# Statistics, weight sums, aggregation, buffer order and top row in a windowed attention followed by a convolution

## The chip, the core and the metric

The kernel runs on one core of a Trainium2 chip. TensorE (PE) multiplies, VectorE (DVE), ScalarE (ACT) and GpSimd (POOL) do the work on elements, SyncE (SP) issues most of the transfers. Each engine takes its instructions in their order and waits for the others by semaphores. [...] The metric is the device time in microseconds, here the median of three runs.

## The reference, cut to what matters

```
x: (2, 128, 256, 256)
# layer 0: halo attention, windows of 8x8 queries, 12x12 keys, 4 heads of 32
x = x + attention(gn(x), W_qkv, W_out, rel_height, rel_width)
# layer 1
n = gn(x)
t1 = conv(n, w1 (128,128,5,1));  t3 = depthwise_conv(t1, w3, 3 rows)
t4 = sum over c and three columns (-2, 0, +2) of n * w4   # 8 groups
x = x + t4 * t3

gn(v): over 32 groups of 4 channels, (v - mean) / sqrt(var + 1e-5),
       mean and var over the group's 4 channels and all 256x256 pixels
```

A normalisation therefore needs the mean and variance of a whole image before its first element can be normalised. There are four: x0 and x1 (the inputs of the two images) and y0 and y1 (their sums after the attention).

## The kernel before, in words

The channels lie on the 128 partitions. An image is cut into 32 strips of 8 rows (`NS`), and the two images make 64 strips k. In the attention a strip is worked on in two units u = 2k and 2k+1, one for each parity of rows, 128 in all (`NU`). In the convolution a strip is one step.

**Setup (L225 to L253).** Constants are loaded, and all 32 strips of the first image come in through six buffers `f_sx`. VectorE takes statistics of each with four `bn_stats` (`Norms.chunk`), one for every two rows, into a table of 128 x 6 numbers. `normalise(0)` (L299) then calls `Norms.group`, which runs `Norms.steps` through: one `bn_aggr` over the whole table, a matmul with `gavg` that averages the channels of a group, small operations on VectorE, a second matmul, a square root on ScalarE and its reciprocal.

**Attention.** From L553 the order on each engine is the order of the program, written by hand. A unit is: biases, scores (L458, L474), values (L439, copied out by ScalarE and VectorE, L445), coefficients of the next strip (L418), attend (L499 to L506), turn (L517), then keys or queries of later units (L354, L393), then project (L533), which adds the input and stores the result from `f_x1` by SP (L537). In even units the next strip is normalised on VectorE (L322 to L328), and GpSimd sorts it into `f_xq` (L337). Every unit also takes statistics of the result before (`result_stats`).

While image 0 is worked on, image 1's input statistics are taken: `stats_at` says which strip in which unit. `load_next` loads it into the single buffer `f_sx`, one ahead, and `input_stats` runs four `bn_stats` at the start of the unit. The steps of a normalisation are spread over two units: `norm_at` starts x1 at u=61 and y0 at u=69, and `step()` runs one piece at a time. At u=8 VectorE prepares six sums of convolution weights (`Weights.sums`, L638).

**Passage to the convolution.** `convolutions_fast` is a generator. The last units of the attention call it for the first loads, the first normalised strip, its row sums and its `unfold` (L735, with five small transfers on SP, L754). Then the attention's pools close: `f_cst` with the constants, keys and values, `f_x1` with two result buffers, `f_wk` with the working tiles. The convolution opens `f_t1` and `f_wk1` on the same addresses. Pools stand one behind the other in the order in which they are opened, so a tile may have to wait for the last use of what lay there.

**Convolution (L894 on).** A strip is: `unfold` (L740) and `first_rows`, then `vertical` twice (L760, L799, results to VectorE L803, L810, L816), with the next strip's normalisation between (L684, L687, L688 on ScalarE, L727, L731 on VectorE), `depthwise` (L828), `spread` (L839) and `combine` (L849). The last image's aggregation y1 starts at k=3. Products go through four banks, `pj`, in turn.

## Time and profile before

| | us |
|---|---|
| median of three runs (3076.55 to 3078.32) | 3078.05 |
| the profiled execution | 3077.89 |
| its span, first to last instruction | 3076.00 |
| PE busy | 2950.9 (96%) |
| DVE busy | 2522.4 (82%) |
| ACT busy | 1732.8 (56%) |
| POOL busy | 657.8 (21%) |
| granted TensorE clock, mean | 0.998 |

The profile lists, for each engine and line, the busy time, and the idle time ahead of an instruction with what ended it. A row of the timeline reads: start, length, engine, line, operation, out<-in, shapes, count, and in brackets the idle time before it with its releaser. Several instructions of a line in succession are merged into one row. A busy TensorE is modelled, so gaps between the starts of the same step in successive units are the safer measure of its delays.

### The profile page before, as it was taken

The numbers are of one execution on the slowest core, as the hardware profiler recorded it, in microseconds if no ns is written. First come the engines' busy times: TensorE is split into PE (matmuls) and PEld (weight loads), VectorE is DVE, ScalarE is ACT, GpSimd is POOL, SyncE is SP. The second block draws the span as 40 slices with busy tenths as digits, with TensorE's granted clock in tenths as the row PEclk, the third lists the DMA queues.
The fourth block names the chain that finished last, engine by engine and source line by source line (L and its number), as shares of the span: only waits on it lengthen the run. The fifth ranks groups of instructions, "written<-read, shape, count | busy, mean of one in ns | idle before, by whom it ended". The sixth has DMA issues, their size and how long they took to land.

```text
span 3076.0 us, 116627 instructions
## 1 busy us (share of the span) xinstructions
PE 2950.9 (96%) x52090; PEld 2223.8 (72%) x52090; DVE 2522.4 (82%) x4092; ACT 1732.8 (56%) x2673; POOL 657.8 (21%) x1433
## 2 busy tenths in 40 slices
PE   0799999999999999999999999999999999999998
PEld 0688888888888888888888888884444444444443
DVE  8788888888888877777777777768999999999998
ACT  0455555555555655555555555555666665666664
POOL 2322232323232222323232323220000000000001
PEclk9999999999999999999999999999999999999999
DMA  9433333333333221222222222225788888888886
GB/s 393 167 126 126 114 117 113 116 113 116 112 117 113 85 72 65 89 72 90 73 90 73 90 72 89 73 96 141 209 222 221 215 210 217 216 217 216 217 216 167
DMA packets 137404, 434.78 MB, mean 141 GB/s; under 512 B 12992, under 2 KB 87616, under 8 KB 104384
## 3 DMA queue, kind: packets, MB, share of 16 engines
q1 hardware_dynamic: 127824, 361.18, 33.8%
q0 software_dynamic: 9072, 66.06, 11.7%
q8 instruction: 412, 6.75, 0.9%
q14 instruction: 96, 0.79, 0.1%
HBM read 284.59 MB, written 134.22 MB: 136 GB/s over the span
## 4 chain that ended last, share of the span: by engine, by line
PE 93%; DVE 2%; ACT 1%; issue 0%; POOL 0%; DMA 0%; SPq 0%; DVEq 0%; ACTq 0%
PE f_pv L439 15%; PE a_e L760 10%; PE a_o L760 10%; PE f_s L474 8%; PE f_o L499 8%; PE f_pk L354 8%; PE f_pq L393 7%; PE f_py L354 7%; PE f_pa L418 4%; PE f_s L458 4%; PE a_d L799 3%; PE b L839 2%; PE a_c L760 2%; PE g L740 2%; POOL f_xq L337 0%
## 5 line engine op out<-in xcount | busy, mean ns | idle before, releaser
L445 DVE COPY f_vt<-f_pv 64x512 f32<-64x512 f32 x512 | 354.2, 695 | 299.5 <-ACT f_vt L445 299.3
L337 POOL COPY f_xq<-f_xn 128x128 f32<-128x128 f32 x1024 | 399.2, 441 | 707.9 <-DVE f_xn L322 647.9
L439 PE MATMUL f_pv<-f_wqkvT,f_xn 128*128 128x128 f32 x4096 | 491.3, 278 | 0.0
L439 PEld LDWEIGHTS f_pv<-f_wqkvT,f_xn 128*128 128x128 f32 x4096 | 466.9, 192 | 8.6
L483 ACT ACTIVATE f_p<-f_s 128x512 f32<-128x512 f32 x512 | 264.5, 602 | 320.0 <-PE f_s L474 320.0
L399 ACT ACTIVATE f_q<-f_pq,f_head 128x512 f32<-128x512 f32 x512 | 303.1, 703 | 145.2 <-PE f_pq L393 145.2
L445 ACT COPY f_vt<-f_pv 64x512 f32<-64x512 f32 x512 | 298.2, 584 | 116.9 <-PE f_pv L439 116.5
L821 ACT ACTIVATE t<-t,w 128x1024 f32<-128x1024 f32 x128 | 146.9, 1148 | 372.4 <-DVE t L816 367.9
L828 DVE SCALAR_TENSOR_TENSOR t<-t,w,t 128x1024 f32<-128x1024 f32 x256 | 329.9, 1288 | 7.4 <-ACT t L821 1.3
L474 PEld LDWEIGHTS f_s<-f_q,f_kt 64*64 64x64 f32 x16384 | 250.9, 135 | 50.1 <-issue 49.9
L474 PE MATMUL f_s<-f_q,f_kt 64*64 64x64 f32 x16384 | 268.7, 220 | 0.6 <-issue 0.6
L367 ACT COPY f_kt<-f_pk 128x512 f32<-128x512 f32 x256 | 154.6, 604 | 196.4 <-PE f_pk L354 196.4
L499 PE MATMUL f_o<-f_vt,f_p 128*32 128x66 f32 x16384 | 263.6, 222 | 1.4 <-issue 0.7
L857 POOL DMA_DIRECT2D y<-f_x x63 | 54.7, 868 | 915.2 <-DVE y L849 900.2
L499 PEld LDWEIGHTS f_o<-f_vt,f_p 128*32 128x32 f32 x16384 | 241.9, 110 | 10.8 <-DVE f_cf L431 1.0
L354 PE MATMUL f_py<-f_ot,f_woT 128*128 128x256 f32 x1024 | 242.2, 379 | 2.2 <-DVE f_ot L517 2.2
L354 PE MATMUL f_pk<-f_xn,f_wqkvT 128*128 128x256 f32 (+2 forms) x1258 | 243.0, 345 | 0.0
L393 PE MATMUL f_pq<-f_xq,f_wq_s 128*128 128x256 f32 (+1 forms) x1370 | 240.5, 331 | 0.8 <-DVE f_rc L505 0.8
L313 POOL COPY f_xn<-f_xn 128x1280 f32<-128x1280 f32 x62 | 86.7, 1399 | 720.6 <-PE f_pv L439 720.6
L760 PE MATMUL a_e<-xm,w1s 128*128 128x512 f32 x512 | 240.7, 591 | 0.0
L760 PE MATMUL a_o<-xm,w1s 128*128 128x512 f32 x512 | 240.3, 590 | 0.0
L393 PEld LDWEIGHTS f_pq<-f_xq,f_wq_s 128*128 128x128 f32 x1370 | 208.2, 191 | 23.3 <-PE pv_x L141 0.4
(131 smaller groups left out, 4696.9 us busy)
## 6 DMA issues: line engine op xcount, KB each, us to landing
f_raw<-in_x SPq DMA_DIRECT2D x62, 1280.0 KB, 7.8
f_sx<-in_x SPq DMA_DIRECT2D x64, 1024.0 KB, 12.4
f_x<-f_x SPq DMA_DIRECT2D x128, 512.0 KB, 3.4
y<-f_x POOLq DMA_DIRECT2D x63, 1024.0 KB, 8.0
out<-y SPq DMA_DIRECT2D x63, 1024.0 KB, 4.4
raw<-f_x SPq DMA_DIRECT2D x64, 640.0 KB, 6.4
raw<-f_x SPq DMA_DIRECT2D x62, 384.0 KB, 6.5
t<-t4p SPq DMA_DIRECT2D x192, 32.0 KB, 4.7
```

The costliest lines, as they stand in the source:

```text
L337: nc.gpsimd.tensor_copy(xq[:, half, t2, :, :, c].rearrange("p t r n e -> p r t n e"), cells[:, :, 16 * half + c : 16 * half + 16 : 2, 1 + ...
L354: nc.tensor.matmul(dst[:, 512 * lo // last : 512 * hi // last], w, moving[:, n * lo // last : n * hi // last], start=True, stop=True,)
L367: nc.scalar.copy(cur[:, c, 1:129, 2:6], pk.rearrange("p (j i) -> p j i", i=4))
L393: nc.tensor.matmul(pq.rearrange("p (h n e t) -> p h t n e", h=2, n=8, e=2)[:, half, lo:hi], wq_s, xq[:, half, :, :, r, c].rearrange("p s t ...
L399: nc.scalar.activation(q[:, c, :, i], pq.rearrange("p (n x) -> p n x", n=NPAIR), AF.Copy, scale=head[:, i : i + 1],)
L439: nc.tensor.matmul(pv[:, P * n : P * n + P], xn[k % 2][:, r, 4 * j + n].rearrange("p c x -> p (c x)"), wvT, start=True, stop=True,)
L445: (nc.vector.tensor_copy if c else nc.scalar.copy)(vt[rows, 4 * j : 4 * j + 4, :, c, 0:32], pv[rows].rearrange("p (n h d) -> p n h d", n=4 ...
L474: nc.tensor.matmul(sc[g][n // 8][64 * c : 64 * c + 64, n % 8].rearrange("p i x -> p (i x)"), keys_k[rows, c, 48 * n : 48 * n + 64], qs[u][ ...
L483: nc.scalar.activation(pts[u][:, g, 8 * half : 8 * half + 8].rearrange("p n i x -> p (n i x)"), sc[g][half].rearrange("p n i x -> p (n i x ...
L499: nc.tensor.matmul(po[32 * h : 32 * h + 32, n - lo], p[:, h // 2, n, h % 2], vt[:, n, h], start=True, stop=True,)
L760: nc.tensor.matmul(pa[:, : n * W], w, rows, start=i == 0, stop=i == len(terms) - 1)
L828: nc.vector.scalar_tensor_tensor(t3[:, j : j + 4], t1[:, j + tap : j + tap + 4, :], w3[:, tap : tap + 1], t3[:, j : j + 4], ALU.mult, ALU.add,
```

## The change

Five edits:

1. Image 1's input statistics are taken in odd units only: ten rows each in the first eight, eight rows in the other twenty-two. Before, two strips fell on the even units 4 and 8. The buffer `f_sx` grows to ten rows. To make room, the first strip's `t4` moves from its own tile into the unused rows of `raws[0, -1]`.
2. The six weight sums run on GpSimd instead of VectorE.
3. The table of statistics is aggregated in four quarters. Three of each image's quarters are aggregated early: in the setup after strips 7, 15 and 23, in the attention at the ends of the units in `quarter_at`. The last is the first step of the normalisation, and the small operations combine the four.
4. The pool of the results, `f_x1`, is opened after the working pool `f_wk`.
5. For the first strip of the convolution the products of the top row are issued right after `unfold(0)`, ahead of the last projection, and their copy stays in `first_rows`.

```diff
@@ class Norms
+    def quarter(self, st, name, i):
+        if i == 0:
+            self.mvs[name] = self.glob.tile([P, 4, 2], F32, tag=f"mv_{name}", name=f"mv_{name}")
+        self.nc.vector.bn_aggr(
+            self.mvs[name][:, i], st[:, self.ns * i : self.ns * i + self.ns].rearrange("p n k -> p (n k)")
+        )
     def steps(self, st, ps_pool, name, tag="pj"):
-        mv = small.tile([P, 2], F32, tag="mv", name=f"mv_{name}")
-        nc.vector.bn_aggr(mv, st.rearrange("p n k -> p (n k)"))
+        self.quarter(st, name, 3)
+        mv = self.mvs[name]
         yield
...
-        nc.tensor.matmul(pm[:, 0:1], gavg, mv[:, 0:1], start=True, stop=True)
+        nc.tensor.matmul(pm[:, 0:4], gavg, mv[:, :, 0], start=True, stop=True)
         yield
...
-        nc.vector.tensor_copy(mean, pm[:, 0:1])
-        d = small.tile([P, 1], F32, tag="d", name=f"d_{name}")
-        nc.vector.tensor_sub(d, mv[:, 0:1], mean)
+        nc.vector.tensor_reduce(mean, pm[:, 0:4], AX.X, ALU.add)
+        nc.vector.tensor_scalar(mean, mean, 0.25, None, ALU.mult)
+        d = small.tile([P, 4], F32, tag="d", name=f"d_{name}")
+        nc.vector.tensor_scalar(d, mv[:, :, 0], mean, None, ALU.subtract)
+        nc.vector.tensor_mul(d, d, d)
+        nc.vector.tensor_add(d, d, mv[:, :, 1])
         q = small.tile([P, 1], F32, tag="q", name=f"q_{name}")
-        nc.vector.tensor_mul(q, d, d)
-        nc.vector.tensor_add(q, q, mv[:, 1:2])
+        nc.vector.tensor_reduce(q, d, AX.X, ALU.add)
...
-        nc.vector.tensor_scalar(v, pv[:, 0:1], 1e-5, None, ALU.add)
+        nc.vector.tensor_scalar(v, pv[:, 0:1], 0.25, 1e-5, ALU.mult, ALU.add)
@@ attention_fast, setup
                 norm.chunk(st_x[0], 4 * s, t)
+                if s % 8 == 7 and s < 31:
+                    norm.quarter(st_x[0], "x0", s // 8)
+        wk = l0.enter_context(tc.tile_pool(name="f_wk", bufs=2))
         x1p = l0.enter_context(tc.tile_pool(name="f_x1", bufs=2))
-        wk = l0.enter_context(tc.tile_pool(name="f_wk", bufs=2))
...
+        quarter_at = {}
         for b in range(NB - 1):
-            for s in range(NS - 2):
-                stats_at[2 * (b * NS + s) + 1] = b + 1, s
-            stats_at[2 * (b * NS + 2)] = b + 1, NS - 1
-            stats_at[2 * (b * NS + 4)] = b + 1, NS - 2
+            row = 0
+            for i in range(NS - 2):
+                n = 10 if i < 8 else 8
+                stats_at[2 * (b * NS + i) + 1] = b + 1, row, n
+                row += n
+            for i, u in enumerate((30, 46, 58)):
+                quarter_at[2 * b * NS + u] = st_x, b + 1, f"x{b + 1}", i
...
+        for b in range(NB):
+            for i, u in enumerate((34, 50, 66) if b + 1 < NB else (34, 42, 50)):
+                quarter_at[2 * b * NS + u] = st_y, b, f"y{b}", i
...
                 project(u)
                 step()
+                if u in quarter_at:
+                    st, i, name, part = quarter_at[u]
+                    norm.quarter(st[i], name, part)
@@ Weights.sums
-        self.nc.vector.tensor_add(self.w1s[:, 0], w[1], w[3])
-        self.nc.vector.tensor_scalar(self.w1s[:, 1], w[3], -1.0, None, ALU.mult)
+        self.nc.gpsimd.tensor_add(self.w1s[:, 0], w[1], w[3])
+        self.nc.gpsimd.tensor_scalar(self.w1s[:, 1], w[3], -1.0, None, ALU.mult)
         for i, (a, b) in enumerate(((2, 1), (4, 3), (0, 1), (2, 3))):
-            self.nc.vector.tensor_sub(self.w1s[:, 2 + i], w[a], w[b])
+            self.nc.gpsimd.tensor_sub(self.w1s[:, 2 + i], w[a], w[b])
@@ convolutions_fast
             if k == 0:
-                t4 = both.sb.tile([P, 2, W], F32, tag="t4", name=f"t4_{k}")
+                t4 = raws[0, -1][:, 0:2, :]
...
+        def top_row(k):
+            xt = xn[k % 2]
+            return taps(
+                f"{k}_first", 1,
+                [(w1[:, tap], xt[:, tap - 1 : tap, 2 : 2 + W]) for tap in (2, 3, 4)],
+            )
-        def first_rows(k):
+        def first_rows(k, top=None):
...
-                top = taps(
-                    f"{k}_first", 1,
-                    [(w1[:, tap], xt[:, tap - 1 : tap, 2 : 2 + W]) for tap in (2, 3, 4)],
-                )
-                nc.scalar.copy(t1[:, 1:2, :], top)
+                nc.scalar.copy(t1[:, 1:2, :], top_row(k) if top is None else top)
...
         unfold(0)
+        top = top_row(0)
         yield
...
-                first_rows(k)
+                first_rows(k, top if k == 0 else None)
```

More of the change, by code (lines that the diff above doesn't have):

```diff
@@ L111, in __init__ @@
         self.nc, self.glob, self.small, self.gavg, self.ns = nc, glob, small, gavg, ns
-        self.done = {}
+        self.done, self.mvs = {}, {}
     def new(self, name, tag):
@@ L274, in load_next @@
                 u = coming.pop(0)
-                b, s = stats_at[u]
-                sxs[u] = t = rawp.tile([P, 8, W], F32, tag="sx", name=f"f_sx_{b}_{s}", bufs=1)
-                nc.sync.dma_start(t, x[b, :, 8 * s : 8 * s + 8, :])
+                b, row, n = stats_at[u]
+                t = rawp.tile([P, 10, W], F32, tag="sx", name=f"f_sx_{b}_{row}", bufs=1)
+                sxs[u] = t[:, 0:n]
+                nc.sync.dma_start(sxs[u], x[b, :, row : row + n, :])
         def input_stats(u):
-            b, s = stats_at[u]
-            norm.chunk(st_x[b], 4 * s, sxs.pop(u))
+            b, row, n = stats_at[u]
+            norm.chunk(st_x[b], row // 2, sxs.pop(u))
         def load_rows(k):
@@ L666, in load_rows1 @@
             if s == 0:
-                pre = rawp.tile([P, 8, W], F32, tag="sx", name=f"raw1_{b}_pre", bufs=1)
+                pre = rawp.tile([P, 10, W], F32, tag="sx", name=f"raw1_{b}_pre", bufs=1)
                 nc.sync.dma_start(pre[:, 5:8, :], x1_d[b][0][:, 0:3, :])
@@ L761, in taps @@
             return pa[:, : n * W].rearrange("p (r w) -> p r w", w=W)
-        def first_rows(k):
+        def top_row(k):
[5 more added lines that the diff above has]
+        def first_rows(k, top=None):
             s = k % NS
-            xt = xn[k % 2]
             t3 = wk.tile([P, 8, W], F32, tag="t3", name=f"t3_{k}")
```

## Prediction

> **What bounds the kernel now.** The page comes first: it gives engine shares and the chain that ended last.

> ```profile
> PE 2950.9 (96%) x52090; PEld 2223.8 (72%) x52090; DVE 2522.4 (82%) x4092; ACT 1732.8 (56%) x2673; POOL 657.8 (21%) x1433
> PE 93%; DVE 2%; ACT 1%; issue 0%; POOL 0%; DMA 0%; SPq 0%; DVEq 0%; ACTq 0%
> ```

> TensorE carries the kernel, and the change removes no matmul. It can gain only where TensorE waits, so the waits and the timeline come next. The first matmuls of L458 mark the starts of the 128 units. Units last 15.31 to 15.35 us except at u=0 (16.49), 4 (16.17), 8 (19.89), 61 (16.87), 62 (18.09), 64 (16.2, four extra matmuls), 69 (16.86), 70 (16.55) and 126 (14.37). In the convolution the first matmuls of L740 mark strips of 15.17 us, except the first (19.68), second (16.84) and fifth (17.14).

> Timeline of u=8, then of odd unit 29, then of u=61:

> ```profile
> 239.43 2.46 DVE L119 BATCH_NORM_STATS2 st_x<-f_sx 128x6 f32<-128x512 f32 x4
> 242.35 1.71 DVE L644 TENSOR_TENSOR w1s<-w 128x128 f32<-128x128 f32 x4
> 244.93 1.88 PE L418 MATMUL f_pa<-f_xq,f_wb 128*64 128x64 f32 x32 [2.95 <-DVE f_vt L445]
> ...
> 562.31 2.46 DVE L119 BATCH_NORM_STATS2 st_x<-f_sx 128x6 f32<-128x512 f32 x4
> 566.54 0.69 DVE L445 COPY f_vt<-f_pv 64x512 f32<-64x512 f32 x1 [1.76 <-ACT f_vt L445]
> ...
> 1061.91 0.15 DVE L133 COPY mean_x<-pm_x 128x1 f32<-128x1 f32 x1
> 1063.53 3.73 PE L393 MATMUL f_pq<-f_xq,f_wq_s 128*128 128x256 f32 x22 [0.38 <-DVE f_rc L505]
> ```

> In even units, which also normalise a strip, VectorE's added work makes TensorE wait. After four statistics an odd unit still has 1.76 us of idle VectorE; without them it has 4.14. At u=61 the small operations stand ahead of f_rc, and the projection waits for them.

> Timelines of the setup and of the passage to the convolution:

> ```profile
> 42.49 47.37 DVE L119 BATCH_NORM_STATS2 f_st_x<-f_sx 128x6 f32<-128x512 f32 x76 [0.48 <-DMA f_sx<-in_x]
> 89.90 3.62 DVE L127 BATCH_NORM_AGGREGATE mv_x<-f_st_x 128x2 f32<-128x768 f32 x1
> ...
> 2083.24 1.96 PE L354 MATMUL f_py<-f_ot,f_woT 128*128 128x256 f32 x8 [1.47 <-DVE f_ot L517]
> 2085.04 1.46 PE L760 MATMUL a_first<-xm,w 128*128 128x256 f32 x6
> 2091.25 0.37 ACT L794 COPY both<-a_c 128x256 f32<-128x256 f32 x1 [4.30 <-DMA f_x<-f_x]
> 2102.36 0.70 PE L760 MATMUL a_c<-sm,w1s 128*128 128x256 f32 x2 [0.90 <-DVE c L803]
> 2141.09 3.61 DVE L127 BATCH_NORM_AGGREGATE mv_y<-st_y 128x2 f32<-128x768 f32 x1
> 2150.28 0.70 PE L760 MATMUL a_c<-sm,w1s 128*128 128x256 f32 x2 [1.31 <-DVE c L803]
> ```

> Setup: 75 steps between 76 statistics take 47.37-0.68 us, 0.623 each; in unit 29 they take (2.46-0.67)/3 = 0.597. So VectorE waits some 4 x 0.026 = 0.10 us per strip for the loads, whose windows show the DMA engines full (419 GB/s). It looks busy but is paced by transfers.

> [...] (1) [...] the smallest take 0.13 to 0.16 us. (2) [...] L828, 2.60 us for two, takes 4.02 beside GpSimd's L870. [...]

> **The change, part by part.** The sum stands against the profiled 3077.89 us (span 3076.00 and 1.89 around it), 0.16 below the median.

> 1. *Statistics in odd units only.* u=4 and u=8 lose 2.46 us of VectorE each. u=4 gains 16.17-15.33 = 0.84. Eight odd units get a fifth statistic, 0.60, under 1.76 of idle: 0 (uncovered, 8 x 0.60 = 4.8). SP loses two loads; the eight of 1.31 MB, 25% longer, are issued a pair of units (30.7 us) ahead, against 12.4 to landing, and the first stands behind the first two strips' rows: 0.

> 2. *Weight sums on GpSimd.* VectorE loses 0.27+0.43+1.71 at u=8. With part 1 its loss goes: 19.89-15.33 = 4.56. GpSimd queues the six ahead of f_xq, behind L313 which ends at 228.13; f_xq starts at 238.12, waiting for normalisation, so 9.99 us stand free. Dear bound: L871, 1.70 us for 256 elements, gives 6 x 1.70 = 10.2, 0.2 too long. [...] I take 0.

> Parts 1 and 2: -5.4.

> 3. *Aggregation in quarters.* By (1) a quarter costs between 3.61/4 = 0.90 and (3.61-0.16)/4+0.16 = 1.02; I take 0.95.
>  - Setup: three quarters go among the statistics. Each delays VectorE by 0.95, and the next eight strips win 0.8 back from its waits; 0.45 is left at the end. The next load is issued up to 1.25 us late, but a load takes 12.4 us to land, five strips of 2.5, so DMA keeps a queue. Then 0.95 replaces 3.62: 0.45+0.95-3.62 = -2.2. Two more small operations follow on the open chain, 0.19 each: +0.4. Sum -1.8. If every delay of VectorE delayed the loads too: 3 x 0.95+0.95-3.62+0.4 = +0.6. The first strip's rows landed at 90.45, so they are not late next.
>  - Attention: three quarters for x1 and six for y close even units; the following odd units' 1.76 or 4.14 cover them: 0 (uncovered, 9 x 0.95 = 8.6). At u=61 and 69 the whole aggregate was hidden (0.61 of idle after it), so shortening gives nothing, but the two extra operations stand ahead of f_rc, for which the projection waits: 2 x 0.4 = +0.8. The square roots at u=62 and 70 keep their loss.
>  - Convolution: the aggregate at 2141.09 cost the fifth strip 17.14-15.17 = 1.97, of which 0.31 is pm's own matmuls. A 0.95 operation stays inside the lead of 1.87 us that VectorE's c has in steady strips (c at 3045.80, a_c at 3047.67): -1.65.

> 4. *Results' buffers behind the others.* `both` is the first tile written in the convolution's working pool. That pool's addresses cover the buffers of f_x1, and its copy L794 starts 0.10 us after the last f_x store landed at 2091.15. By the tiles' sizes (45 KB of constants, 50 of wk, 8 of x1; 39 of t1, sm and df, 43 of wk1) the new pools end before x1's new place. L794 then follows a_c, near 2085.7. Behind it on ScalarE stand L684, L687 and L688, 5.0 us, done near 2091; VectorE's sums start after its t at about 2092.3 instead of 2096.63. TensorE's banks are then free in time.

> 5. *Top row early.* a_first's 1.30 us go into TensorE's wait of 1.47 for f_ot. Its bank holds one of four until ScalarE copies it, near 2083.5; the next user a_d comes at 85.5. No DMA moves; the new home of t4 changes nothing timed.

> Parts 4 and 5 together: the first a_c comes at 2085.04 instead of 2086.34, then 14.06 us to the next L740 as now, then a strip of 15.17: 2114.27 against 2117.24, so -3.0 (1.30 from the row, 16.84-15.17 = 1.67 from the buffers).

> Sum: -5.4-1.8+0.8-1.65-3.0 = -11.0, so 3066.9; with 0.16 to the median, **3067 us**.

> **Rivals.**
>  - *A: setup gains nothing.* The loads are paced by VectorE's releases: +0.6 instead of -1.8, 3069.4. For: each load is issued within 0.1 us of a strip's end. Against: five are queued.
>  - *B: `both` still waits.* Another landing or tile holds it. Then VectorE is as late as now, the early row is spent in a longer wait at 2102.36, and parts 4 and 5 give nothing: 3070. For: the wait is inferred, and takes in several semaphores. Against: the 0.10 us.
>  - *C: odd units have no room.* Statistics and quarters pass through: +4.8+8.6, 3080.4, within the measurement. Against: 1.76 us of idle in every odd unit.
>  - *D, slower: a quarter costs as much as a whole.* Setup: 3 x 3.61, less 2.4 won back in 24 strips, plus 0.4 = +8.8. The five quarters of the first image cost 3.61-1.76 = 1.85 each, +9.3. The fifth strip keeps its loss. Then -5.4+0.8+8.8+9.3-3.0 = +10.5: 3088.5. It decides from some 2.6 us per quarter. For: only the whole was ever run. Against: (1), and 0.67 for 512 elements of statistics.

> **How the numbers follow.** 0.2% is 6.2 us, about what a measurement can tell from no change: faster is under 3071.9, slower over 3084.2. Chances: forecast 0.64 (own range 3063.5 to 3070), A 0.12, B 0.10, C 0.07, D 0.04, a larger gain 0.03. Nearly all of forecast, A and the gain, and most of B, are faster: 0.85; C and the remainder are same, 0.11; D slower, 0.04. From 3063 to 3071.5 holds the forecast, A and most of B, 0.83.

> **What would show it.** Right: u=4, 8 and odd units up to 15 at 15.33; quarters of 0.95; the first normalisation at 95.3 instead of 97.16; u=61 and 69 at 17.3; L794 within 1 us of a_c; second strip 15.2, fifth 15.5. Wrong: quarters above 1.5 us, odd units beyond 15.5, L794 still at a landing, or GpSimd's sums running past 238.

## The result and the profile after

The changed kernel takes 3067.0 us (median; 3066.32 to 3068.80) against 3077.98 (3076.55 to 3078.65) measured beside it: ratio 0.9966, 95% interval 0.9954 to 0.9977. That is -11.0 us, as forecast. The profiled execution took 3068.38 us (span 3066.58), 9.43 us of span less than before; it stands 1.4 above the median, and most of that lies at u=62, where something happened that no step of the prediction named. Two of the twelve executions of one later kernel, the one with the order of the pools undone, ran at a mean granted clock of 0.64 and 0.66 and took 5227 and 4359 us; its median leaves them out.

The page after, engine shares and chain by engine:

```profile
PE 2950.1 (96%) x52090; PEld 2223.6 (73%) x52090; DVE 2521.1 (82%) x4106; ACT 1733.1 (57%) x2673; POOL 659.7 (22%) x1439
PE 95%; DVE 1%; ACT 0%; POOL 0%; issue 0%; POOLq 0%; DVEq 0%; ACTq 0%
```

TensorE has the same 52090 matmuls and busy time; its part of the chain rises from 93 to 95%, VectorE's falls from 2 to 1. The gain lies in waits alone. By units and strips (the starts of L478 and of L763, which were L458 and L740):

| place | before | after | difference | predicted |
|---|---|---|---|---|
| start of u=0 | 110.45 | 108.45 | -1.99 | -1.8 |
| u=4 | 16.17 | 15.34 | -0.83 | -0.84 |
| u=8 | 19.90 | 15.34 | -4.56 | -4.56 |
| u=61, u=69 (each) | 16.87 | 17.32 | +0.45 | +0.4 |
| u=62 | 18.09 | 20.02 | +1.93 | 0 |
| first strip | 19.67 | 18.38 | -1.29 | -1.30 |
| second strip | 16.85 | 15.16 | -1.69 | -1.67 |
| fifth strip | 17.14 | 15.39 | -1.75 | -1.65 |
| eighth strip | 15.56 | 15.22 | -0.34 | 0 |

Timeline after, GpSimd in u=7 and 8:

```profile
225.25 0.45 POOL L664 TENSOR_TENSOR w1s<-w 128x128 f32<-128x128 f32 x1
225.68 0.53 POOL L665 TENSOR_SCALAR w1s<-w 128x128 f32<-128x128 f32 x1
226.19 1.69 POOL L667 TENSOR_TENSOR w1s<-w 128x128 f32<-128x128 f32 x4
...
235.18 3.37 POOL L357 COPY f_xq<-f_xn 128x128 f32<-128x128 f32 x8 [7.31 <-DVE f_xn L342]
```

The six sums take 2.63 us and are done 7.31 us before GpSimd's next work, which waits for VectorE: nothing is behind them. Odd units with five statistics last 15.31 to 15.32; VectorE's idle time ahead of their first f_vt fell from 1.76 to 1.17, and to 0.89 after a quarter.

Timeline after, setup, passage and fourth strip, the places that the prediction showed of before:

```profile
90.07 1.02 DVE L127 BATCH_NORM_AGGREGATE mv_x<-f_st_x 128x2 f32<-128x192 f32 x1
95.20 3.35 DVE L342 TENSOR_SCALAR f_xn<-f_raw,mean_x,rstd_x 128x640 f32<-128x640 f32 x4
...
2077.28 1.56 PE L783 MATMUL a_first<-xm,w 128*128 128x256 f32 x6
2080.63 0.59 PE L783 MATMUL a_c<-sm,w1s 128*128 128x256 f32 x2
2081.26 0.37 ACT L820 COPY both<-a_c 128x256 f32<-128x256 f32 x1 [1.96 <-PE a_c L783]
2133.71 1.01 DVE L127 BATCH_NORM_AGGREGATE mv_y<-st_y 128x2 f32<-128x192 f32 x1
```

One quarter of 1.02 stands where 3.62 stood, though three more were added ahead of it. From the end of the last statistics to the first normalisation it is now 5.16 us, and was 7.30. That is the safer measure of the setup: the last statistics themselves end anywhere between 88.40 and 90.19 in the fourteen traces of this case, with early quarters and without, and u=0 moves with them. The copy of `both` (L794 before) follows its product by 0.04 us and no longer waits for a DMA landing.

Now u=62, where 1.93 us were lost. Timeline, and then a table of windows (columns: busy time and instructions of PE, PEld, DVE, ACT, POOL, then granted clock, DMA share, GB/s):

```profile
1064.78 0.13 DVE L168 TENSOR_SCALAR less_x<-mean_x 128x1 f32<-128x1 f32 x1
1065.31 3.36 DVE L342 TENSOR_SCALAR f_xn<-f_raw,mean_x,rstd_x 128x640 f32<-128x640 f32 x4 [0.40 <-issue]
1070.43 0.79 PE L438 MATMUL f_pa<-f_xq,f_wb 128*64 128x64 f32 x18 [1.48 <-DVE f_vt L465]
1071.58 0.76 PE L438 MATMUL f_pa<-f_xq,f_wb 128*64 128x64 f32 x14 [0.36 <-POOL f_xq L357]
1072.27 3.54 PE L519 MATMUL f_o<-f_vt,f_p 128*32 128x66 f32 x128
```

```profile
1068.64:1072.05 3.41, 1.57 (x35) 1.27 (x34) 3.35 (x7) 0.99 (x2) 3.41 (x10) 1.00 0.21 84
1072.05:1075.46 3.41, 3.41 (x122) 3.29 (x122) 2.00 (x6) 0.78 (x1) 2.98 (x9) 0.50 0.02 5
1075.46:1078.87 3.41, 3.41 (x36) 2.90 (x27) 3.18 (x7) 1.40 (x3) 0.00 (x0) 1.00 0.02 5
```

The kernel before, at the same place:

```profile
1077.11 0.80 PE L418 MATMUL f_pa<-f_xq,f_wb 128*64 128x64 f32 x18 [1.12 <-DVE f_vt L445]
```

Two things happen. VectorE starts the normalisation 0.40 us late, with no wait that the profile shows (before: 0.04 between the two), so TensorE's wait for f_vt grows from 1.12 to 1.48. And in the window after those waits TensorE's clock is at half: L519 takes 3.54 us instead of 2.05. The kernel before has this too, at u=8, after the wait of 2.95 us that the prediction showed; the same table of that kernel:

```profile
241.67:245.08 3.41, 0.46 (x8) 0.30 (x9) 3.38 (x9) 0.69 (x2) 3.41 (x10) 1.00 0.79 277
245.08:248.50 3.42, 3.42 (x96) 3.30 (x98) 2.37 (x5) 0.78 (x1) 0.99 (x3) 0.50 0.35 134
```

So the change takes away one half-rate window, and in the profiled execution got another. At both places the clock is at 0.50 for 3.413 us. All starts of such windows lie a whole number of 3.413 us from each other and from the place near the kernel's beginning where the clock becomes full (a product of 128x256 takes 0.63 us ahead of it and 0.38 behind it): 245.08-101.72 = 42 x 3.413 before the change, 1072.05-99.25 = 285 x 3.413 after it. So within an execution the grid of the windows is fixed. Of the bound these two traces tell only that 1.84 us of idle time within one window, 54% of it, was enough, and that 1.47 us (43%, at 2081.46 in the kernel before) was not. The experiments had to find it.

### The profile page after: what moved, and what is told of

Same layout as the page of the kernel before. It is cut to its first block, busy times and chain, and to the rows that moved or that the text cites. A ratio compares the mean times of both kernels' runs of the same rounds, so it can differ in the third digit from the quotient of the medians.

```text
span 3066.6 us, 116700 instructions
## 1 busy us (share of the span) xinstructions
PE 2950.1 (96%) x52090; PEld 2223.6 (73%) x52090; DVE 2521.1 (82%) x4106; ACT 1733.1 (57%) x2673; POOL 659.7 (22%) x1439
## 4 chain that ended last, share of the span: by engine, by line
PE 95%; DVE 1%; ACT 0%; POOL 0%; issue 0%; POOLq 0%; DVEq 0%; ACTq 0%
PE f_pv L459 15%; PE a_e L783 11%; PE a_o L783 11%; PE f_s L494 8%; PE f_o L519 8%; PE f_pk L374 8%; PE f_pq L413 8%; PE f_py L374 7%; PE f_pa L438 4%; PE f_s L478 4%; PE a_d L825 4%; PE b L865 2%; PE a_c L783 2%; PE g L763 2%; POOL f_xq L357 0%; ACT f_q L419 0%
## 5 line engine op out<-in xcount | busy, mean ns | idle before, releaser
L519 PE MATMUL f_o<-f_vt,f_p 128*32 128x66 f32 x16384 | 264.3, 222 | 0.8 <-DVE f_cf L451 0.7
L519 PEld LDWEIGHTS f_o<-f_vt,f_p 128*32 128x32 f32 x16384 | 242.6, 110 | 10.2 <-DVE f_cf L451 1.0
```

Source lines behind the costliest of these rows:

```text
L519: nc.tensor.matmul(po[32 * h : 32 * h + 32, n - lo], p[:, h // 2, n, h % 2], vt[:, n, h], start=True, stop=True,)
```

## The experiments

**Each of the two first parts alone.** Two kernels from the one before. In one the weight sums go to GpSimd (`self.nc.vector` to `self.nc.gpsimd` in `sums`). In the other the statistics go to odd units:

```diff
-            for s in range(NS - 2):
-                stats_at[2 * (b * NS + s) + 1] = b + 1, s
-            stats_at[2 * (b * NS + 2)] = b + 1, NS - 1
-            stats_at[2 * (b * NS + 4)] = b + 1, NS - 2
+            row = 0
+            for i in range(NS - 2):
+                n = 10 if i < 8 else 8
+                stats_at[2 * (b * NS + i) + 1] = b + 1, row, n
+                row += n
...
-                t4 = both.sb.tile([P, 2, W], F32, tag="t4", name=f"t4_{k}")
+                t4 = raws[0, -1][:, 0:2, :]
```

The last edit comes along because ten rows take 2 KB more per partition than eight, as much as t4 took in its own tile.

> The kernel before with only the statistics moved to the odd units (t4 of the first strip shares the buffer of the first rows, which makes the room for ten rows). Theory of slack and clock: an even unit has some 1.6 us of spare VectorE time, and at u=8 the wait of 2.95 us also filled most of one 3.41 us window of the TensorE clock, which then ran at half rate for the next window (1.6 us of loss). u=4 falls from 16.17 to 15.34; u=8 keeps the sums, 2.41 us of VectorE, waits under 1 us and keeps the clock: 16.1 (from 19.90, so -3.8). No half-rate window there. Sum -4.6. Rival, the VectorE time counts one for one: u=8 falls by 2.46 only, to 17.4, sum -3.3.

> The kernel before with only the six weight sums moved to GpSimd. Theory of slack and clock: u=4 stays at 16.17, u=8 becomes a second u=4: 16.17 (-3.7) with no half-rate window; so either part alone brings most of the 4.56 at u=8, and the two are not additive. Rival, the VectorE time counts one for one: u=8 at 17.5 (-2.4).

Measured: with odd units alone u=4 is 15.34 and u=8 16.24 (3073.64 us, ratio 0.9988, 0.9981 to 0.9995); with GpSimd alone u=4 is 16.17 and u=8 16.21 (3073.63, ratio 0.9989, 0.9982 to 0.9996). Neither has a half-rate window before the end. So each alone brings 3.7 of the 4.56 at u=8, the second only 0.9 more. The totals fall by 3.8 each, where 4.6 and 3.7 were expected. The first 2.4 us taken from VectorE there shortened TensorE's wait by about 2.1 (from 2.95 to 0.82 and 0.80) and saved the clock, 1.6; what was left of the load fits into the unit's slack but for 0.9. The one-for-one rival (17.4) is out.

**Undoing the order of the pools, and the early row.** Two kernels from the changed one.

```diff
-        wk = l0.enter_context(tc.tile_pool(name="f_wk", bufs=2))
         x1p = l0.enter_context(tc.tile_pool(name="f_x1", bufs=2))
+        wk = l0.enter_context(tc.tile_pool(name="f_wk", bufs=2))
```

> The changed kernel with the pool of results opened ahead of the working pool again. Theory of the prediction: the copy of `both` stands at the landing of the last f_x store again, some 5 us after a_c; the first two strips together take 36.5 us as before (33.54 in the changed kernel), because the early top row is then only spent in a longer wait: +3.0. Rival 1, the two parts are independent: +1.67 (second strip 16.85, first strip 18.4). Rival 2, the order of the pools does nothing: 0, and `both` stays within 1 us of a_c. u=62 of this and of every run on the changed kernel: 18.1 to 18.5 where its wait leaves less than half of a clock window idle, 20.0 where it leaves more.

The two strips take 18.96 and 18.89 us: 37.85, so +4.3. Timeline of this kernel:

```profile
2079.08 0.59 PE L783 MATMUL a_c<-sm,w1s 128*128 128x256 f32 x2
2085.29 0.37 ACT L820 COPY both<-a_c 128x256 f32<-128x256 f32 x1 [7.52 <-DMA f_x<-f_x]
2090.67 1.23 DVE L750 TENSOR_TENSOR sm<-xm 128x1024 f32<-128x1024 f32 x1 [2.89 <-ACT xm L711]
```

The copy waits for the landing of f_x again, 5.6 us behind its product, ScalarE's normalisation behind it is late, and VectorE's sums wait 2.89 for that, as in the kernel before. The mechanism is the predicted one. The size is 1.3 above +3.0: TensorE then idles 1.70 us in the window 2094.26 to 2097.68, and the next runs at half rate. The time is 3070.26 (ratio 0.9977, 0.9968 to 0.9986), +3.3 on the changed kernel. In this profile u=62 has nearly the same waits as in the changed kernel (1.54 and 0.36) but takes 18.49: there the grid lay across the waits, with at most 1.38 us in one window, and the clock stayed.

```diff
-        top = top_row(0)
...
-                first_rows(k, top if k == 0 else None)
+                first_rows(k)
```

> The changed kernel with the top row's products back behind the opening of the pools. Theory of the prediction: the first strip is longer by a_first's 1.30 us (18.38 to 19.68), the second stays at 15.2: +1.3. Rival: the copy of `both` and ScalarE's work behind it set the end of the first strip, and the row is hidden: 0.

The first strip takes 19.67, the second 15.17: +1.29 and +0.01, the predicted term. The time is 3068.16 (ratio 0.9971, 0.9960 to 0.9982), 1.2 more than the changed kernel. In this execution u=62 had the half-rate window (20.05).

**The quarters of the setup.** First they were only moved in the program, behind the last statistics:

```diff
                 norm.chunk(st_x[0], 4 * s, t)
-                if s % 8 == 7 and s < 31:
-                    norm.quarter(st_x[0], "x0", s // 8)
+            for i in range(3):
+                norm.quarter(st_x[0], "x0", i)
```

> The changed kernel with the first image's three early quarters taken out from among the setup's statistics and put behind the last of them. Theory of the prediction: VectorE wins back nearly all of a quarter's 1.02 us in the eight strips that follow, since those strips wait some 0.1 us each for their loads; three quarters at the end stand open, so the first normalisation and all behind it come 3 x 1.02 less the 0.26 us of lag that is left = 2.8 us later. Rival, the loads pace the setup and were delayed by the quarters themselves: the strips land 1 us earlier per quarter taken out, and the difference is under 0.5 us.

3066.98 us, and the first normalisation at 95.25: no difference. But the trace has the quarters at 29.74, 50.13 and 70.12 again, as in the changed kernel. The setup is not ordered by hand; the built program has each aggregate where its data are ready. The edit did nothing, so this run says nothing of the cost. But every engine's instructions in it are those of the changed kernel, one by one, so its trace is a second execution of that kernel: u=62 takes 18.48 there, its waits lie across two windows (1.49 us idle in the fuller one), no window runs at half rate, and the span is 3064.85, 1.73 less. So 1.54 of the 1.73 us between two executions of one program lies at u=62. The second kernel lays the statistics out so that each quarter of them contains one of the last strip's four:

```diff
-                norm.chunk(st_x[0], 4 * s, t)
-                if s % 8 == 7 and s < 31:
-                    norm.quarter(st_x[0], "x0", s // 8)
+                for c in range(4):
+                    n = 4 * s + c
+                    norm.chunk(st_x[0], n + n // 31 if n < 124 else 32 * c + 31, t[:, 2 * c : 2 * c + 2])
+            for i in range(3):
+                norm.quarter(st_x[0], "x0", i)
```

> The changed kernel with the first image's statistics laid out so that each quarter of them holds one of the last strip's four: no quarter can be aggregated before the last strip's statistics, whatever order is chosen for the setup. Theory of the prediction: the three quarters, 3 x 1.02 us, now stand open behind the loads, less the 0.2 us by which they had delayed the last statistics: the first normalisation comes 2.8 us later than in the changed kernel, at 98.0 instead of 95.20, and u=0 with it. Rival, the loads pace the setup and were delayed by the quarters themselves: under 0.5 us.

Timeline of VectorE in this kernel:

```profile
89.78 3.65 DVE L127 BATCH_NORM_AGGREGATE mv_x<-f_st_x 128x2 f32<-128x192 f32 x4
97.53 3.39 DVE L344 TENSOR_SCALAR f_xn<-f_raw,mean_x,rstd_x 128x640 f32<-128x640 f32 x4
```

The first normalisation is 2.33 us later than in the changed kernel, u=0 starts 2.39 later. Counted from the last statistics it is 2.50 later (7.66 instead of 5.16). Four quarters in a row overlap and take 3.65, not 4 x 1.02, which is why it is less than 2.8. What three quarters placed early cost the last statistics can't be told from nothing: they end at 89.24 to 90.19 in the nine traces that have them and at 88.40 to 89.96 in the five without. Three whole quarters would be 3.06 us, so VectorE wins most of it back; that it does so from its waits for loads is the prediction's account, and fits. The rival "setup gains nothing" is out.

**What brings the half rate: doses.** In 20 even units VectorE gets extra work on constant data, to make waits of chosen length:

```diff
+                for i in range(DOSE.get(u, 0)):
+                    nc.vector.bn_stats(spare, weights.w1[:, 0:4].rearrange("p a b -> p (a b)"))
                 if u in stats_at:
```

> The changed kernel with extra statistics on constant data, whose results nothing reads, at the head of 20 even units: 4 (3 units), 5 (7 units), 6 (7 units) or 7 (3 units) of 0.60 us each. Each unit has 1.6 us of spare VectorE time, so TensorE's wait is some 0.8, 1.4, 2.0 or 2.6 us. Theory of the clock: the clock is judged in windows of 3.41 us whose grid runs on by itself; it falls to half rate for one window where a window was idle for half of it or more. Waits of 0.8 never bring it (unit 16.2); of 2.6 in most cases (unit 19.5 to 20); 1.4 and 2.0 bring it only where the wait lies in one window and not across two, and then the unit is 1.5 to 1.7 us longer than an equal unit without it. Rival, each wait above a certain length brings it wherever the grid stands: units of one dose are all alike. Second rival, the slow products at u=62 come from something else there, such as GpSimd's copies: no half-rate window in the dosed units.

| extra statistics | TensorE's wait | most idle time in one window | clock after it | units | time of the unit |
|---|---|---|---|---|---|
| 4 | 1.14 to 1.20 | 1.14 to 1.20 | full | 3 | 16.55 to 16.62 |
| 5 | 1.87 to 1.97 | 1.16 to 1.70 | full | 5 | 17.28 to 17.38 |
| 5 | 1.90, 1.99 | 1.90, 1.99 | half | 2 | 18.91, 19.01 |
| 6 | 2.67 | 1.54 | full | 1 | 18.08 |
| 6 | 2.59 to 2.69 | 2.21 to 2.69 | half | 6 | 19.39 to 19.66 |
| 7 | 3.36 | 1.81 | full | 1 | 18.78 |
| 7 | 3.39, 3.42 | 2.33, 2.51 | half, two windows | 2 | 21.40, 21.50 |

Timelines of TensorE at u=76 (six extra statistics) and u=110 (five):

```profile
1326.07 1.15 PE L442 MATMUL f_pa<-f_xq,f_wb 128*64 128x64 f32 x32 [2.67 <-DVE f_vt L469]
1327.15 2.05 PE L523 MATMUL f_o<-f_vt,f_p 128*32 128x66 f32 x128
...
1869.62 1.15 PE L442 MATMUL f_pa<-f_xq,f_wb 128*64 128x64 f32 x32 [1.90 <-DVE f_vt L469]
1870.70 3.46 PE L523 MATMUL f_o<-f_vt,f_p 128*32 128x66 f32 x128
```

Where the grid lies, and not the length of the wait, decides: the wait of 1.90 brought the half rate, the one of 2.67 did not. What counts is the idle time within one window. In this and the other traces up to 1.64 us (48%) never brought it and 1.84 (54%) and more always did; at 1.70 it came once and stayed away once, and at 1.81 it stayed away. So the bound in these traces is close to half a window, and neither rival holds. With its wait taken off, a dosed unit lasts 15.4 us at the full clock, 16.7 to 17.0 with one half-rate window and 18.0 to 18.1 with two: a price of 1.3 to 1.6 us per window. The theory of one half-rate window per idle one is not the whole of it: the second half-rate window of the last two units follows a window, itself at half rate, in which TensorE was idle for only 1.07 and 0.92 us. What brings the full clock back no run isolates.

**Filling the wait.** Three products that nothing reads, in the changed kernel's wait at u=62:

```diff
                 for j in range(4):
                     values(u, j)
+                if u == 62:
+                    for i in range(3):
+                        nc.tensor.matmul(
+                            sc[1][1].rearrange("p n i x -> p (n i x)")[:, 0:256], wkT,
+                            wqkvT[:, 0:256], start=True, stop=True, skip_group_check=True,
+                        )
```

> The changed kernel with three products of 256 columns added at u=62 (into a bank of scores that is free then, read by nothing), at the place where TensorE waits 1.48 us for f_vt. Theory of the clock: the wait that is left is under 0.5 us, no window is half idle, the products of u=62 run at full rate, and u=62 takes 18.5 instead of 20.0: the kernel with three products more is as fast as the fastest runs of the changed kernel. Rival, work is work: u=62 takes 20.0 plus 1.4.

u=62 takes 18.46, with at most 0.56 us idle in a window and no half rate: as expected there. The total was not: 3068.24 (ratio 0.9970, 0.9958 to 0.9981), no better than the changed kernel. Ten even units from u=72 to 124 had become 0.08 to 0.71 us longer, 3.5 us in all. Timeline in one of them, u=80:

```profile
1357.77 2.46 PE L374 MATMUL f_pk<-f_xn,f_wqkvT 128*128 128x256 f32 x12 [0.40 <-issue]
```

TensorE stood still for 0.40 us in the midst of one product's parts, waiting for nothing that the trace shows. The three products, far ahead of it, are six matmuls and six weight loads in the trace and had moved all that follows by twelve places. It looks like the 0.40 us that VectorE shows at u=62, which led to the next two runs. The five longest of the ten units have such a stop, of 0.13 to 0.40. In the fourteen traces all 34 stops of TensorE of 0.15 us and more from u=1 on that no wait explains lie two or three places past a multiple of 64, counted in order of start with weight loads and waits. They are nine different places. Two of these have it in 13 and 14 of the traces, in this one too, where twelve instructions more stand ahead of them.

**The place in the program.** In the changed kernel and all built on it so far but one, the normalisation at u=62 starts at place 1728 of VectorE's program (waits that are instructions of their own are counted), and has the 0.40 us. In the kernel before it stands at 1722, in the one with doses at 1784, and there it has none. Six sets of one element in u=3, which has time to spare, move it in the kernel before; three move it in the changed one:

```diff
+                for _ in range(6 if u == 3 else 0):
+                    nc.vector.memset(spare, 0.0)
                 if u in stats_at:
```

> The kernel before with six sets of one element added on VectorE in u=3, which has 1.76 us to spare; nothing reads them. At u=62 of every kernel on the changed one the first instruction of the normalisation stands at place 1728 of VectorE's program and starts 0.40 us after the one before it, with no wait that the profile shows; in the kernel before it stands at 1722, in the run with the doses at 1784, and starts at once. Theory of the place: the added six bring it to 1728, and the 0.40 us appear in this kernel too, so u=62 goes from 18.09 to 18.5 (20.0 if the clock's window then lies on the wait). Rival, the quarters or the two additional small operations cause it: u=62 stays at 18.1, with no idle time ahead of the normalisation.

> The changed kernel with three sets of one element added on VectorE in u=3, which bring the first instruction of u=62's normalisation from place 1728 to 1731. Theory of the place: the 0.40 us go, u=62 takes 18.1 and no window of the clock is half idle there. Rival: u=62 takes 18.5, or 20.0 with the half-rate window, as in the changed kernel.

Timeline of the kernel before with six sets, then of the changed kernel with three:

```profile
1070.21 0.13 DVE L158 TENSOR_SCALAR less_x<-mean_x 128x1 f32<-128x1 f32 x1
1070.74 3.41 DVE L323 TENSOR_SCALAR f_xn<-f_raw,mean_x,rstd_x 128x640 f32<-128x640 f32 x4 [0.40 <-issue]
1075.92 0.78 PE L419 MATMUL f_pa<-f_xq,f_wb 128*64 128x64 f32 x18 [1.53 <-DVE f_vt L446]
1078.11 3.16 PE L500 MATMUL f_o<-f_vt,f_p 128*32 128x66 f32 x128
```

```profile
1064.07 0.13 DVE L168 TENSOR_SCALAR less_x<-mean_x 128x1 f32<-128x1 f32 x1
1064.25 3.40 DVE L343 TENSOR_SCALAR f_xn<-f_raw,mean_x,rstd_x 128x640 f32<-128x640 f32 x4
```

With six sets and no part of the change, the kernel before has the 0.40 us, 1.89 us of idle time in one window, the half rate and u=62 at 20.03. With three sets the changed kernel has neither; u=62 takes 18.12, its value before. So the quarters and the two additional small operations have no part in it: the change happened to put this instruction on a place where VectorE pauses. Each of the two kernels ran once (3078.61 and 3065.40 us), so the reading rests on the traces and not on these times. 1728 is 27 x 64, and some other multiples of 64 do the same. In the changed kernel VectorE's sum L836 of the convolution begins 0.46 us after the operation ahead of it at places 3520, 3648 and 4672, which are 55, 57 and 73 x 64, and 0.10 to 0.14 at all others from the second strip on. The first of them:

```profile
2247.46 0.69 DVE L836 TENSOR_TENSOR t<-a_e,c 128x512 f32<-128x512 f32 x1 [0.46 <-PE b L865]
```

The place alone is not enough. Most multiples of 64 show no such delay, and at place 1728 itself another instruction, in the kernel before and in the changed kernel with three sets, begins 0.03 us after the one ahead of it. What VectorE does there stays open.

The eighth strip's 0.34 goes with the quarters and not with the place: it takes 15.22 in all ten traces that have quarters, with three sets too, and 15.56 or 15.57 in three of the four without. VectorE is still 0.41 us behind there from the long aggregation: its c of the seventh strip starts 0.99 us ahead of that strip before the change, 1.40 after it. With six sets it takes 15.94, by a pause of 0.37 at place 3392, 53 x 64.

**A better kernel.** u=61, 62, 69 and 70 still lose time to the normalisations' steps. These were begun a unit earlier and spread over two units, with an exponential behind the square root that brings ScalarE's table back where ScalarE is idle (each exchange of the table takes 1.28 us in the traces: in the changed kernel one at 1062.39 for the square root and one at 1064.33 for the next exponential):

```diff
-            norm_at[2 * (b * NS + NS - 2) + 1] = st_x, b + 1, f"x{b + 1}"
-            norm_at[2 * ((b + 1) * NS + 2) + 1] = st_y, b, f"y{b}"
+            norm_at[2 * (b * NS + NS - 2)] = st_x, b + 1, f"x{b + 1}"
+            norm_at[2 * ((b + 1) * NS + 2)] = st_y, b, f"y{b}"
...
+                turns = (1, 6, 7) if u in norm_at else (2, 2, 3, 7) if u - 1 in norm_at else ()
+                place = iter(range(1, 8))
+
+                def step():
+                    for _ in range(turns.count(next(place))):
+                        next(steps)
```

> The changed kernel with the steps of the normalisations spread over two units and begun one unit earlier (x1 at u=60 and 61, y0 at u=68 and 69): the last quarter ahead of u=60's scores, the mean after its projection, the variance after u=61's values, the square root behind u=61's coefficients where ScalarE is idle for 4 us, with one exponential after it that brings its table back, the reciprocals at the end of u=61. Theory: the losses at u=61, 62, 69 and 70 are waits for round trips and for the exchange of ScalarE's tables, not work that has no room. Then u=60, 61, 68 and 69 take 15.7 each (a product with one column more each), u=62 and 70 15.34, and no clock window is half idle at u=62: 93.4 us for these six units where the changed kernel takes 101.9 with the half-rate window and 100.3 without, so -6.9 to -8.5. Rival, the exchange of tables only moves: the queries of u=61 and 69 wait for ScalarE, both stay at 17.3, and the gain is 4 or less.

3061.22 us, ratio 0.9947 (0.9930 to 0.9963), 5.8 less than the changed kernel. u=60, 61, 68 and 69 take 15.57, 15.44, 15.57 and 15.44, u=70 15.38. The six units sum to 94.7, 7.1 less than with the half-rate window and 5.6 less than without: short of the expectation by 1.3, because u=62 takes 17.32. That unit also computes the second image's first keys (1.04 us), which the expectation left out, and its normalisation is still late:

```profile
1061.76 0.13 DVE L170 TENSOR_SCALAR less_x<-mean_x 128x1 f32<-128x1 f32 x1
1062.29 3.38 DVE L344 TENSOR_SCALAR f_xn<-f_raw,mean_x,rstd_x 128x640 f32<-128x640 f32 x4 [0.40 <-issue]
```

The next kernel puts the reciprocals ahead of u=61's sums and one pair of result statistics off by a unit:

```diff
-                if u > 0:
+                if u > 0 and not late:
                     result_stats(u - 1)
...
+                if u - 2 in norm_at and norm_at[u - 2][0] is st_x:
+                    result_stats(u - 2)
                 step()
                 attend(u)
```

> The kernel with the steps spread over two units, with the second image's reciprocals ahead of u=61's projection sums and the statistics of u=60's result put off from u=61 to u=62, behind its coefficients. In the spread kernel u=62 takes 17.32, of which 1.04 are the first keys of the second image; its normalisation starts 1.3 us later than VectorE's sums of u=61 end (six small operations, then 0.40 of idle). Theory: the normalisation follows the sums at once, u=62 falls to 16.4, and the kernel gains 0.9 on the spread one: some 3060.3. Rival: the reciprocals or the later statistics delay the sums, so the gain moves into u=61 or u=62: 0.

3060.68 us, ratio 0.9944 (0.9928 to 0.9961); u=62 is 17.14. The normalisation does follow at once, at 1061.12, and TensorE no longer waits for f_vt. But the statistics that were put off now stand on VectorE ahead of f_rc, so 0.2 is gained in the unit instead of 0.9: the rival. The intervals of the two kernels can't be told apart. In every execution both are faster than the changed kernel in any of its own (3061.64 at most against 3066.32 at least).

## Why the prediction was right, step by step

- **Parts 1 and 2** (-5.4): right to 0.01. What the prediction did not see is what the 4.56 at u=8 is made of: a wait of 2.95 us and some 1.6 of half-rate clock that followed it. It took the whole excess over 15.33, so the clock was counted without being named. Its row already showed it: L418 took 1.88 us there for 32 matmuls, where it takes 1.15 elsewhere.
- **Part 2's price on GpSimd**: 2.63 us for the six sums, under the dear bound of 10.2 and within the 9.99 that stood free, so the 0 was right. The trace of before showed only the dear bound, which was 0.2 too long; that the sums would fit was the author's estimate.
- **Part 3, setup** (-1.8): measured -1.99 at u=0, and -2.14 behind the last statistics, where the prediction's terms without the lag give -2.27. The quarter took 1.02, the upper of the two bounds, where 0.95 was chosen. (Both were estimates from the whole aggregate's 3.61 us, the upper one with the 0.16 us of VectorE's smallest operations as a part that does not shrink.) The lag of 0.45 that the three early ones were to leave is smaller than what the setup varies by, so that -1.99 lies so near -1.8 says little.
- **Part 3, attention** (+0.8): measured +0.91, the two small operations ahead of f_rc. The quarters cost nothing in odd units.
- **The step that failed** is "The square roots at u=62 and 70 keep their loss". At u=70 it held (16.55 to 16.52). At u=62 it was +1.93 in the profiled execution: 0.4 from the pause at place 1728, 1.5 from the half-rate window that the longer wait brought. Where the grid lies otherwise it is +0.4 (18.48 to 18.49 in three other traces, one of them of the same instructions). This explains why the profiled sum is -9.4: in the second execution of the same instructions, without the half-rate window, it is -11.2. That the median met the forecast to 0.1 is partly luck: +0.4 at u=62, and in some executions 1.5 more, against -0.34 in the eighth strip, -0.2 in the setup and -0.1 in the fifth.
- **Part 3, convolution** (-1.65): measured -1.75. The quarters there were not undone by a run of their own, but the fifth strip takes 15.39 or 15.40 in all ten traces that have them and 17.14 in the four without.
- **Parts 4 and 5** (-3.0): measured -1.29 and -1.69, and each shown by undoing it. As rival B argued, without the buffers the row's gain is spent in a longer wait: the two strips then take 37.85, 1.3 more than before the change, with a half-rate window among it.
- **Rivals.** A: out by the 2.14 behind the last statistics and by the held quarters. B: out by 0.04 us between product and copy (that the wait takes in several semaphores is in the trace of before: L794 has four semaphore instructions, all between 2086.6 and 2091.2). C: out, 15.32. D: out, 1.02 per quarter against its 2.6.

## What to carry to other kernels

A wait of TensorE had two prices here: its length, and 1.3 to 1.6 us more where it left about half of a 3.41 us window of the clock idle (1.84 us and more always brought the half rate, up to 1.64 never, and between the two it came once in three). Short waits add up within a window (1.48 and 0.36 us at u=62), so cutting a wait can save more than its length (at u=8 2.1 us of wait and 1.6 of clock), and a pause of 0.40 us on VectorE brought the half rate at u=62. When a small edit moves a place that it doesn't touch, shift the instructions by a few cheap ones before looking for a cause in the edit. Before removing work from a full engine, ask whether it is work or waits for round trips: spreading the same steps over two units gained 5.8 us, up to 1.5 of it a half-rate window, where shortening the aggregation there gained nothing.
